# A two-layer graph attention kernel: the attention products ahead of the scores in each turn

## The chip, the cores and the metric

The kernel runs on one core of a Trainium2 chip. The metric is the device time of one execution in microseconds (us); the median of several runs is used. Every core has the same engines: TensorE (PE in the profile; its weight loads are listed as PEld), VectorE (DVE), ScalarE (ACT), GpSimd (POOL) and SyncE (SP), which issues all the transfers here. Each engine works through its own list of instructions in order, and semaphores tie the lists together.

## The reference

The input x holds 128 graphs of 128 nodes with 512 features, in fp32; adj is a Boolean adjacency matrix for each graph. Two layers follow one another, each with a residual and a layer norm:

```
x = layernorm(x + attention0(x, adj))                    # 4 heads of 64, q/k/v from x, output Wo and bias
x = layernorm(x + attention1(layernorm'(x), adj | eye))  # 8 heads of 64, pre-norm with gamma, beta
```

In both, attention is softmax(mask(q k^T / 8)) v for each head, and then the output projection. Masked positions get a very negative value.

## The kernel before

**Work and turns.** The graphs are taken in 64 groups of two (`G = 2`). The groups pass through a software pipeline: `step(s)` is one turn, and holds work of five groups at once. In turn s, layer 0 makes q, k and v for group s (`product_0`), masks and softmaxes the scores of group s-1 ("part 0"), multiplies the probabilities of group s-2 with its values and makes its output projection (`out_product(0, s-2, ...)`); layer 1 makes q and k for s-2 (`qk`) and v for s-3 (`v`), softmaxes the scores of s-3 ("part 1" and "part 2", one for each of its two graphs), and makes the attention product and the output projection of group s-4 (`out_product(1, s-4, ...)`). The full set of this work stands in the turns s = 4 to 63; `opening`, two `closing` turns and `last` surround them.

**The order is written by hand.** The kernel is in manual-schedule mode: each engine executes its instructions in the order in which the calls stand in `step`. So the place of a call in `step` decides what an engine does next, and what stands behind an instruction that waits.

**Products.** All large projections use a scheme of seven products in place of eight (numbered 1 to 7 in `product`, `product_0` and `out_product`). Sums of input halves are made on GpSimd (`halves_sums`, L285). Several products accumulate in the same bank one after another, and after each one the partial sum is read by another engine. The table that says where each number goes:

```
INTO = {1: ("a", True), 2: ("c", True), 6: ("a", False), 5: ("f", True), 7: ("a", False),
        4: ("a", False), 3: ("f", False)}
```

Products 1, 6, 7 and 4 share one bank, 5 and 3 share another, 2 has one of its own. In `product_0` (matmuls at L378), products 1, 6 and 5 are copied away by ScalarE (L387), product 4 by ScalarE too (L389), and 2, 7 and 3 are added by VectorE (L392). In `out_product` (matmuls at L416) every product is added into the residual row r by VectorE (L420), and the next product of that bank must wait for this read. The `qk` and `v` products (L322) are handled by `taken` (ScalarE L348 and L350, VectorE L353).

**Banks.** PSUM, where TensorE writes, has eight banks here: four in a rotating pool (`mm_tile`, tag "mm"), and four with fixed tags: "a", "f", "a0" and "f0". `product_0` uses a0 and f0; `qk` and `v` use a and f; `out_product` uses a and f in layer 0, a0 and f0 in layer 1. Before the change, part 1 of the scores is written to a0 and f0, and the attention products of parts 0 and 1 to a and f.

**Softmax.** `scores` makes the score matmuls of all three parts (L449, L455; 64 active rows of the array). `masked` copies them to tiles that hold the mask's value (VectorE, L483), `maxima` takes the maxima of the rows (VectorE, L489), `exps` the exponentials with their sums (ScalarE, L498, four heads to a call for one half), `normalised` the reciprocals (VectorE, L506) and the scaling (GpSimd, L507). `blocks` and `probs_arrive` transpose the probabilities through VectorE (L522) and a trip to memory and back (L197, L203). `attend` multiplies them with the values (L568; 64 active columns) and copies the product to the tile aT (ScalarE, L571 and L573).

**Norms.** `stats` collects mean and variance on VectorE (L600, L601), `roots` computes the scale and the shift on GpSimd (L608 to L623), and appends the norm itself (ScalarE, L634) to a list; `flush()` in `step` emits what is on the list. `turn` transposes the normed rows for layer 1, again through VectorE (L212) and memory; the fetched tile is finished by ScalarE (L251). For layer 0 the same is done with the input, finished in `in_order` (ScalarE, L239).

Of the kernel before, what the change touches and what calls it, by code (L numbers as in the profile page):

```python
# [10 lines left out]
F32 = mybir.dt.float32  # L11
# [6 lines left out]
P = 128  # L18
# [9 lines left out]
def kernel(ctx: ExitStack, tc: tile.TileContext, x, adj, wq, wk, wv, wo, bo,  # L28
# [16 lines left out]
    ps_st = ctx.enter_context(tc.tile_pool(name="ps_st", bufs=1, space=PSUM))  # L45
# [4 lines left out]
    def mm_tile(name):  # L50
        return ps_mm.tile([P, 512], F32, tag="mm", name=name)
# [4 lines left out]
    def flush(what=later):  # L56
        while what:
            what.pop(0)()
# [16 lines left out]
    def load(g):  # L75
        if g >= NG:
            return
        R[g] = six.tile([P, G, E], F32, tag="r", name=f"r_{g}")
        M[g] = six.tile([P, G, N], U8, tag="m", name=f"m_{g}")
        nc.sync.dma_start(R[g], x[g * G:(g + 1) * G].rearrange("b n e -> n b e"))  # L80
        nc.sync.dma_start(M[g], adj[g * G:(g + 1) * G].rearrange("b i j -> i b j"))
# [191 lines left out]
    def sums(l, g):  # L273
        if not 0 <= g < NG:
            return
        xs = XS[l, g] = one.tile([P, 4, KH, N], F32, tag=f"xs{l}", name=f"xs{l}_{g}")
        halves_sums(xs, XT[l, g].rearrange("p (h c) (b n) -> p b h c n", h=2, b=2))

    def halves_sums(xs, a):
        s1, s2, s3, s4 = (xs[:, i] for i in range(4))  # L280
        for o, a0, a1, op in ((s1, a[:, 1, 0], a[:, 1, 1], ALU.add),
                              (s2, s1, a[:, 0, 0], ALU.subtract),
                              (s4, a[:, 0, 1], s2, ALU.subtract),
                              (s3, a[:, 0, 0], a[:, 1, 0], ALU.subtract)):
            nc.gpsimd.tensor_tensor(o, a0, a1, op=op)  # L285
# [142 lines left out]
    def group_of(s, part):  # L428
        g = s - (3 if part else 1)
        return g if 0 <= g < NG else None  # L430

    def scores(s):

        made = {}
        for part in PARTS:
            g = group_of(s, part)
            if g is None:
                continue
            if part == 1:
                ps = [ps_st.tile([P, 512], F32, tag=t, name=f"sc{part}_{g}_{t}") for t in ("a0", "f0")]  # L440
            else:
                ps = [mm_tile(f"sc{part}_{g}_{i}") for i in range(2)]
            ps = [x.rearrange("p (k n) -> p k n", n=N) for x in ps]
            if part == 0:
                for b in range(G):
                    for h in range(HEADS[0]):
                        r = slice((h % 2) * D, (h % 2 + 1) * D)
                        q_, k_ = (QKV[g][r, b, h // 2, i, :] for i in range(2))
                        nc.tensor.matmul(ps[h % 2][:, b * K0 + h // 2, :], q_, k_, start=True, stop=True)  # L449
            else:  # L450
                t = slice((part - 1) * N, part * N)
                for h in range(HEADS[1]):
                    r = slice((h % 2) * D, (h % 2 + 1) * D)
                    q_, k_ = (QK[1, g][r, i * K1 + h // 2, t] for i in range(2))
                    nc.tensor.matmul(ps[h % 2][:, h // 2, :], q_, k_, start=True, stop=True)  # L455
            made[part] = ps
        return made
# [13 lines left out]
    def masked(made, s, *parts):  # L471
        for part in parts:
            g = group_of(s, part)
            if g is None:
                continue
            for i in range(2):
                if part == 0:
                    mask = M[g][:, :, None, :].to_broadcast([P, G, K0, N])
                    o, sc = (x.rearrange("p (b k) n -> p b k n", b=G) for x in (SM[0][:, i], made[0][i]))
                else:  # L480
                    mask = M[g][:, part - 1, None, :].to_broadcast([P, K1, N])
                    o, sc = SM[part][:, i], made[part][i]
                nc.vector.copy_predicated(o, mask, sc)  # L483
# [8 lines left out]
    def exps(s, part, *halves):  # L492
        if group_of(s, part) is None:
            return
        sm, nmax, total = SM[part], NMAX[part], TOTAL[part]
        for i in halves:
            for k in range(K1):
                nc.scalar.activation(sm[:, i, k, :], sm[:, i, k, :], AF.Exp, bias=nmax[:, i, k:k + 1],  # L498
                                     accum_out=total[:, i, k:k + 1])
# [45 lines left out]
    def attend(s, *parts):  # L545

        for part in parts or PARTS:
            l = min(part, 1)
            g = s - (2, 4)[l]
            if not 0 <= g < NG:  # L550
                continue
            K = (K0, K1)[l]
            if part != 2:
                AT[l, g] = one.tile([P, G, K, N], F32, tag=f"aT{l}", name=f"aT{l}_{g}")
            pT = PT.pop((g, part))
            if part == 2:
                pm = mm_tile(f"av{part}_{g}")
            else:
                pm = ps_st.tile([P, 512], F32, tag="af"[part], name=f"av{part}_{g}")
            pm = pm.rearrange("p (k n) -> p k n", n=N)  # L560

            for b in range(G) if l == 0 else (part - 1,):
                for h in range(HEADS[l]):
                    i, kk = h % 2, h // 2
                    at = b * K0 + kk if l == 0 else kk
                    v = (QKV[g][:, b, kk, 2, i * D:(i + 1) * D] if l == 0
                         else V[1, g][:, b, h * D:(h + 1) * D])
                    nc.tensor.matmul(pm[i * D:(i + 1) * D, at, :].rearrange("p (a r) -> p a r", r=32), v,  # L568
                                     pT[:, :, i * K1 + at, :], start=True, stop=True)
            if l == 0:  # L570
                nc.scalar.copy(AT[l, g].rearrange("p b k n -> p (b k) n"), pm)  # L571
            else:
                nc.scalar.copy(AT[l, g][:, part - 1], pm)  # L573
# [155 lines left out]
    def step(s):  # L729

        direct = s in (2, 3)
        made = scores(s)
        load(s + 1)
        if s > 2:
            in_order(s)
            sums(0, s)
        masked(made, s, 0, 1, 2)
        attend(s)
        maxima(s, 0)
        if s > 3:  # L740
            maxima(s, 1)
        out_sums(0, s - 2)
        exps(s, 0, 0)
        product_0(s, 1)
        exps(s, 0, 1)
        out_product(0, s - 2, 1, 2, 5)
        if s == 3:
            maxima(s, 1)
        maxima(s, 2)
        product_0(s, 2)  # L750
        normalised(s, 0)
        out_product(0, s - 2, 6, 3)
        exps(s, 1, 0)
        stats(0, s - 2, 0)
        product_0(s, 6)
        exps(s, 1, 1)
        out_product(0, s - 2, 7)
        product_0(s, 5)
        out_product(0, s - 2, 4)
        stats(0, s - 2, 1)  # L760
        exps(s, 2, 0)
        product_0(s, 7)
        exps(s, 2, 1)
        normalised(s, 1)
        product_0(s, 3)
        blocks(s, 0)
        flush()
        product_0(s, 4)
        if direct:
            prepare(len(setup))  # L770
        else:
            turn(1, s - 2)
        out_sums(1, s - 4)
        v(s - 3, 1, 2)
        out_product(1, s - 4, 1)
        if not direct:
            arrive(1, s - 2)
        blocks(s, 1)
        probs_arrive(s, 0)
        v(s - 3, 6, 5)  # L780
        out_product(1, s - 4, 2)
        normalised(s, 2)
        v(s - 3, 7, 3)
        turn(0, s + 1)
        v(s - 3, 4)
        flush(latest)
        cleared(s + 1, 0, 1)
        if direct:
            finish_direct(s - 2)
        else:  # L790
            finish(s - 2, 0)
        if s == 2:
            weight_sums(w1qk, wsqk, 1)
        out_product(1, s - 4, 6, 5)
        if not direct:
            finish(s - 2, 1)
        out_product(1, s - 4, 7, 3, 4)
        blocks(s, 2)
        probs_arrive(s, 1)
        stats(1, s - 4, 0)  # L800
        stats(1, s - 4, 1)
        arrive(0, s + 1)
        probs_arrive(s, 2)
        cleared(s + 1, 2)
        addend(0, s - 1)
        with_self(s - 2)
        qk(s - 2, 1, 2, 6)
        flush()
        qk(s - 2, 5)
        addend(1, s - 3)  # L810
        qk(s - 2, 7, 3, 4)
        if s == 2:
            weight_sums(w1v, wsv, 0, 1)
        if s == 3:
            weight_sums_out(1)
# [130 lines left out]
```

## Time and profile before

| | before |
|---|---|
| time, median of 3 runs | 2787.71 us (2786.65 to 2788.02) |
| span of the profiled execution | 2784.5 us |
| TensorE matmuls, busy | 2768.7 us (99%) |
| TensorE weight loads, busy | 2609.6 us (94%) |
| VectorE, busy | 1795.3 us (64%) |
| GpSimd, busy | 1747.4 us (63%) |
| ScalarE, busy | 1502.0 us (54%) |
| transfers | 405.24 MB, mean 146 GB/s |
| granted TensorE clock | 1.000 |

How to read it: a busy share is the time in which an engine executed something, over the span. Matmuls overlap one another, so their busy time says that TensorE had work, not that it was at its peak. The timeline lists an engine's instructions by start time, merged where equal ones follow one another; "x16" counts hardware records, of which each fp32 matmul here has two. A bracket at the end of a row gives the idle time ahead of it and whose work ended it. The list of waits sums such idle times by pairs.

### The profile page before, as it was taken

The page shows a single profiled execution, that of the slowest core. Times are in us where ns is not written, and L with a number is a line of the kernel's source. Part 1 is how long each engine was busy: PE and PEld are TensorE (multiplying, and loading weights), DVE is VectorE, ACT ScalarE, POOL GpSimd, SP SyncE. Part 2 cuts the span into 40 slices and gives each one's busy share as a digit, 9 for nine tenths or more (in the row PEclk, how much of TensorE's full clock was granted, in tenths as well). Part 3 has the DMA queues.
Part 4 walks back from the last instruction along what each step waited for, and adds up shares of the span by engine and source line. Part 5 has one row for each costly group of instructions (what it writes and reads, how often), then busy time and mean ns, then how long its engine had stood idle before and what let it go on. Part 6 is the DMA issues. An engine that isn't in the chain of part 4 may idle for free.

```text
span 2784.5 us, 63222 instructions
## 1 busy us (share of the span) xinstructions
PE 2768.7 (99%) x23317; PEld 2609.6 (94%) x23317; DVE 1795.3 (64%) x3307; ACT 1502.0 (54%) x4811; POOL 1747.4 (63%) x2307
## 2 busy tenths in 40 slices
PE   8999999999999999999999999999999999999998
PEld 8999999999999999999999999999999999999997
DVE  5766666666666666666666666666666666666665
ACT  3555555645555556455555564555555645555554
POOL 4566566666665666666656666666566666666664
PEclk9999999999999999999999999999999999999999
DMA  5355454464454544645545445455454464554532
GB/s 169 109 144 165 129 165 148 127 176 140 143 165 128 166 148 127 179 137 143 164 127 168 147 129 175 139 145 165 127 167 146 129 177 135 147 163 128 160 107 69
DMA packets 281796, 405.24 MB, mean 146 GB/s; under 512 B 44680, under 2 KB 206480, under 8 KB 281488
## 3 DMA queue, kind: packets, MB, share of 16 engines
q1 hardware_dynamic: 281488, 401.20, 49.2%
q8 instruction: 185, 3.03, 0.5%
q14 instruction: 123, 1.01, 0.1%
HBM read 205.00 MB, written 196.08 MB: 144 GB/s over the span
## 4 chain that ended last, share of the span: by engine, by line
PE 96%; DVE 1%; issue 0%; POOL 0%; DMA 0%; ACT 0%; SPq 0%; POOLq 0%; ACTq 0%; DVEq 0%
PE qka L322 16%; PE a L378 12%; PE oa L416 12%; PE qkf L322 8%; PE va L322 8%; PE av L568 6%; PE f L378 6%; PE of L416 6%; PE qkc L322 4%; PE vf L322 4%; PE c L378 3%; PE oc L416 3%; PE sc L449 2%; PE sc L455 2%; PE vc L322 2%; PE sc_a L455 2%
## 5 line engine op out<-in xcount | busy, mean ns | idle before, releaser
L507 POOL TENSOR_TENSOR sm<-sm,rec 128x1024 f32<-128x1024 f32 x192 | 364.1, 1896 | 383.1 <-DVE rec L506 382.7
L498 ACT ACTIVATE sm<-sm,nmax 128x128 f32<-128x128 f32 x1536 | 595.4, 394 | 4.6 <-DVE nmax L489 3.7
L589 POOL TENSOR_TENSOR r<-r,bias 128x1024 f32<-128x1024 f32 x128 | 302.2, 2361 | 63.5 <-ACT r L588 63.5
L420 DVE TENSOR_TENSOR r<-oa,r 128x256 f32<-128x256 f32 x508 | 212.1, 418 | 200.3 <-PE oa L416 192.7
L285 POOL TENSOR_TENSOR xs<-xT 128x256 f32<-128x256 f32 x256 | 188.7, 737 | 218.3 <-ACT xT L239 165.1
L498 ACT ACTIVATION_READ_ACCUMULATOR sm<-sm,nmax 128x1 f32 x1536 | 295.9, 193 | 0.0
L348 ACT COPY eqk<-qka 128x512 f32<-128x512 f32 x128 | 74.9, 585 | 349.2 <-PE qka L322 349.2
L483 DVE COPY_PREDICATED sm<-m,sc 128x512 f32<-128x512 uint8 x256 | 172.8, 728 | 135.4 <-PE sc L449 134.9
L322 PE MATMUL qka<-xs,wsqk 128*128 128x128 f32 x2048 | 249.7, 275 | 0.1
L322 PE MATMUL qkf<-xs,w 128*128 128x128 f32 x2048 | 249.8, 275 | 0.0
L522 DVE STREAM_TRANSPOSE turnedp<-sm 128x1024 f32<-128x1024 f32 x189 | 233.9, 1238 | 15.2 <-DMA scrp<-turnedp 10.9
L322 PEld LDWEIGHTS qka<-xs,wsqk 128*128 128x128 f32 x2048 | 239.0, 192 | 0.3 <-POOL xs L285 0.3
L322 PEld LDWEIGHTS qkf<-xs,w 128*128 128x128 f32 x2048 | 239.0, 192 | 0.0
L353 DVE TENSOR_TENSOR qk<-qka,eqk 128x512 f32<-128x512 f32 x64 | 44.3, 691 | 290.4 <-PE qka L322 290.4
L489 DVE TENSOR_REDUCE nmax<-sm 128x8 f32<-128x1024 f32 x192 | 226.2, 1205 | 0.1
L416 PE MATMUL oa<-wso,so 128*128 128x256 f32 x760 | 206.0, 380 | 0.7 <-DVE r L420 0.7
L416 PE MATMUL of<-wo,so 128*128 128x256 f32 x760 | 205.5, 379 | 0.0
L608 POOL TENSOR_SCALAR ve<-mv 128x2 f32<-128x2 f32 x191 | 41.0, 214 | 261.5 <-DVE mv L601 255.4
L634 ACT ACTIVATE r<-r,shift,root 128x512 f32<-128x512 f32 x254 | 192.4, 807 | 8.7 <-POOL shift L623 4.7
L469 POOL MEMSET sm<- 128x1024 f32 x192 | 178.8, 951 | 0.0
L600 DVE BATCH_NORM_STATS2 st<-r 128x6 f32<-128x512 f32 x254 | 171.6, 676 | 4.4
L416 PEld LDWEIGHTS of<-wo,so 128*128 128x128 f32 x760 | 144.2, 190 | 19.9
(155 smaller groups left out, 6801.4 us busy)
## 6 DMA issues: line engine op xcount, KB each, us to landing
scrp<-turnedp SPq DMA_DIRECT2D x189, 512.0 KB, 3.2
pT<-scrp SPq DMA_DIRECT2D x756, 128.0 KB, 4.0
scr<-turned SPq DMA_DIRECT2D x121, 512.0 KB, 4.4
raw<-scr SPq DMA_DIRECT2D x484, 128.0 KB, 3.6
r<-in_x_dram SPq DMA_DIRECT2D x64, 512.0 KB, 3.9
out_dram<-r SPq DMA_DIRECT2D x63, 512.0 KB, 4.9
m<-in_adj_dram SPq DMA_DIRECT2D x64, 32.0 KB, 3.6
raw_r<-in_L_gnn_w_qkv_dram SPq DMA_DIRECT2D x8, 256.0 KB, 4.1
```

What stands on the lines that cost most here:

```text
L285: nc.gpsimd.tensor_tensor(o, a0, a1, op=op)
L322: nc.tensor.matmul(o, lhsT, rhs, start=first and n == 0, stop=n == len(todo) - 1, skip_group_check=True)
L378: nc.tensor.matmul(acc[:, t * P:(t + 1) * P], lhsT, rhs, start=first and n == 0, stop=n == len(todo) - 1, skip_group_check=True)
L416: nc.tensor.matmul(acc, left[:, c], right[:, c], start=first and c == 0, stop=c == hk - 1, skip_group_check=True)
L420: nc.vector.tensor_add(part, acc, part)
L469: nc.gpsimd.memset(sm, NEG1 if part else NEG0)
L489: nc.vector.tensor_reduce(NMAX[part], SM[part], AX.X, ALU.max, negate=True)
L498: nc.scalar.activation(sm[:, i, k, :], sm[:, i, k, :], AF.Exp, bias=nmax[:, i, k:k + 1], accum_out=total[:, i, k:k + 1])
L507: nc.gpsimd.tensor_tensor(SM[part], SM[part], rec[:, :, :, None].to_broadcast([P, 2, K1, N]), op=ALU.mult)
L522: nc.vector.transpose(t.rearrange("p q (h r) -> p q h r", r=32), SM.pop(part).rearrange("p i k (q r) -> p q (i k) r", r=32))
L589: nc.gpsimd.tensor_tensor(R[g], R[g], (bias0, bias1)[l][:, None, :].to_broadcast([P, G, E]), op=ALU.add)
L634: nc.scalar.activation(R[g][:, b], R[g][:, b], AF.Identity, bias=shift[:, b:b + 1], scale=root[:, b:b + 1])
```

## The change

Three edits:

1. In `step`, `attend(s)` is moved ahead of `scores(s)`. On TensorE the attention products of a turn then come first, and the scores after them. `load`, `in_order` and `sums` move ahead of both; `masked` stays behind `scores`. `opening`, `closing` and `last` keep their order.
2. The fixed banks are exchanged to go with it: part 1 of the scores goes to a and f, the attention products of parts 0 and 1 go to a0 and f0. That applies to all turns.
3. The last four exponentials of part 2, `exps(s, 2, 1)`, move from ahead of `normalised(s, 1)` to behind `flush()`. On ScalarE the norm of layer 0's rows (L634) then stands ahead of these four exponentials, and the copy of `product_0`'s fourth product (L389) still stands behind both.

The aim of the first two is to have the attention products, and with them the copies to aT and the sums made of those, early in the turn; the aim of the third is to have the norm's rows early for the transposition that follows.

```diff
@@ scores @@
             if part == 1:
-                ps = [ps_st.tile([P, 512], F32, tag=t, name=f"sc{part}_{g}_{t}") for t in ("a0", "f0")]
+                ps = [ps_st.tile([P, 512], F32, tag=t, name=f"sc{part}_{g}_{t}") for t in "af"]
@@ attend @@
-                pm = ps_st.tile([P, 512], F32, tag="af"[part], name=f"av{part}_{g}")
+                pm = ps_st.tile([P, 512], F32, tag=("a0", "f0")[part], name=f"av{part}_{g}")
@@ step @@
         direct = s in (2, 3)
-        made = scores(s)
         load(s + 1)
         if s > 2:
             in_order(s)
             sums(0, s)
+        attend(s)
+        made = scores(s)
         masked(made, s, 0, 1, 2)
-        attend(s)
         maxima(s, 0)
...
         exps(s, 2, 0)
         product_0(s, 7)
-        exps(s, 2, 1)
         normalised(s, 1)
         product_0(s, 3)
         blocks(s, 0)
         flush()
+        exps(s, 2, 1)
         product_0(s, 4)
```

## The prediction

> **What bounds the kernel now.** I read the page first, then the list of who waited for whom on TensorE, then the timeline of one turn in the steady middle (turn s starts at 1437.20 us, the next at 1480.04: a period of 42.84 us), engine by engine. Columns of the timeline: start, duration, engine, line, operation, count, and in brackets the idle time before it with its releaser.
>
> ```profile
> PE 2768.7 (99%) x23317; PEld 2609.6 (94%) x23317; DVE 1795.3 (64%) x3307; ACT 1502.0 (54%) x4811; POOL 1747.4 (63%) x2307
> PEld a L378 <- ACT aT L573: 10.3, 60, 0.2
> ```
>
> The second line is the longest of the waits: 10.3 us in all, 60 times, 0.2 us at most. TensorE is never short of work: nothing it waits for in the middle of the run exceeds 0.2 us, so the time is that of its instruction list. The change adds and removes no work there. It can gain only what TensorE idles, and it can lose wherever it makes TensorE wait. The slack of the other engines therefore decides.
>
> ```profile
> 1437.20 1.16 PE L449 MATMUL sc<-qkv 64*128 64x128 f32 x16
> 1440.08 1.09 PE L568 MATMUL av<-pT,qkv 128*64 128x128 f32 x16
> 1442.85 1.16 PE L378 MATMUL a<-xT,w 128*128 128x128 f32 x8
> 1446.92 0.60 PE L416 MATMUL oa<-wso,so 128*128 128x256 f32 x2
> 1447.36 0.59 PE L416 MATMUL of<-wo,so 128*128 128x256 f32 x2
> 1449.13 0.60 PE L416 MATMUL oa<-wso,so 128*128 128x256 f32 x2
> 1450.90 0.60 PE L416 MATMUL oa<-wso,aT 128*128 128x256 f32 x2
> 1457.08 1.03 PE L416 MATMUL oa<-wo,aT 128*128 128x256 f32 x4
> ```
>
> The turn opens with scores (2.88 us to 1440.08), then the attention products (2.77 us to 1442.85), then layer 0's products in fixed order. Products 6, 3, 7 and 4 of the layer-0 output (starts 1446.92, 1447.36, 1449.13, 1450.90) reuse two banks, so each needs VectorE to have read the former partial sum. The last row is layer 1's first output product, which needs bank a0.
>
> ```profile
> 1438.45 1.36 DVE L483 COPY_PREDICATED sm<-m,sc 128x512 f32<-128x512 uint8 x2 [2.23 <-PE sc L449]
> 1442.15 2.34 DVE L489 TENSOR_REDUCE nmax<-sm 128x8 f32<-128x1024 f32 x2
> 1444.99 0.42 DVE L420 TENSOR_TENSOR r<-oa,r 128x256 f32<-128x256 f32 x1 [0.50 <-PE oa L416]
> 1446.19 1.21 DVE L489 TENSOR_REDUCE nmax<-sm 128x8 f32<-128x1024 f32 x1
> 1447.89 0.37 DVE L420 TENSOR_TENSOR r<-oa,r 128x256 f32<-128x256 f32 x1
> 1449.76 0.42 DVE L420 TENSOR_TENSOR r<-oa,r 128x256 f32<-128x256 f32 x1
> 1451.53 0.42 DVE L420 TENSOR_TENSOR r<-oa,r 128x256 f32<-128x256 f32 x1 [1.35 <-PE oa L416]
> ```
>
> This is what the page's 64% hides. From the first scores (1438.45) to 1450.18 VectorE works without a pause but for 0.50 us: six masked copies, two maxima, then reads of the output banks. Its share is low over the turn, but here it is a queue with little to spare.
>
> ```profile
> 1452.99 0.19 POOL L608 TENSOR_SCALAR ve<-mv 128x2 f32<-128x2 f32 x1 [3.04 <-DVE mv L601]
> 1454.33 0.22 POOL L623 TENSOR_SCALAR shift<-shift 128x2 f32<-128x2 f32 x1
> 1454.75 1.51 ACT L634 ACTIVATE r<-r,shift,root 128x512 f32<-128x512 f32 x2
> 1456.16 0.46 ACT L389 COPY qkv<-a 128x384 f32<-128x384 f32 x1
> ```
>
> ScalarE reaches the norms (L634) at the moment when the shift that they need is there (1454.55), because eight exponentials filled the time until then. L389, which frees bank a0, follows them.
>
> **What the Trainium skill says.** "PSUM — Partial Sum Buffer", section "Engine vs sequencer instructions", says "ScalarE/VectorE/GpSimdE queues are strict FIFO" and that matmuls start in program order. The trace agrees: each engine's rows stand in the order of the code. So an operation that waits holds back everything behind it. "TensorEngine Tiling (Array Packing)", section "Key Properties", says "Mode switching requires drain". The trace agrees: starts lie 0.112 us apart within full-array matmuls, but 0.205 us apart across the step to the half-row scores.
>
> **The change part by part.**
>
> *Order on TensorE.* Scores and attention products swap places. The work is the same, and there are three mode switches a turn before and after. Extra time over the steady spacing, from the starts of the first instructions after each: full to rows 0.19 us, rows to columns 0.13, columns to full 0.19, sum 0.51. After: full to columns 0.14 (seen in the last turn), rows to full 0.19 (seen once in the opening), columns to rows unseen. I bound that by 0.1 and 0.3 and take 0.19, as for the other switch into rows: sum 0.52. I count it as nothing (at the ends, -0.1 to +0.1 us a turn).
>
> *Banks.* Part 1's scores move from a0/f0 to a/f, the attention products the other way. Banks a and f are free by 1437.9, when ScalarE's copy L350 has read a, and a0/f0 since layer 1's last output read. New waits: oa (1444.29) for the masked copy of part 1, and a0's next product for ScalarE's aT copy. With all of VectorE's masks shifted as below, bank a is read by 1443.2, in time, and the aT copy ends near 1439.5. The last scores share a buffer with the last attention product; its copy ends near 1440.8, before they start. The attention products also need the probabilities 2.88 us sooner: the last fetch is issued by 1475.68 and lands 4.0 us later (median), 1479.7, against 1481.9. All hidden.
>
> *Masks behind the attention products.* The first scores now come 2.77 us later, so VectorE starts at 1441.22 instead of 1438.45, and idles until then. All its following work stays in the same order: masks 3.70 us to 1444.92, two maxima 2.34 to about 1447.18 (an overlap of 0.08 off). Then three reads, no longer waiting for TensorE: starts 1447.18, 1447.66, 1448.00, and the third maximum at 1448.33, 2.14 later than before. The reads behind it keep their distances to that maximum (1.70 us and 3.57 us): product 6's at 1450.03, product 7's at 1451.90. A TensorE wait released by VectorE ends about 0.06 us after the read (from the closing turns, where 2736.46 released 2736.52). So:
> - product 6: 1447.60 + 0.06 = 1447.66, 0.74 late;
> - product 3: 1448.42 + 0.06, 1.12 late;
> - product 7: 1450.40 + 0.06, 1.33 late;
> - product 4: 1452.32 + 0.06 = 1452.38, 1.48 late.
>
> These are totals, not to be added. A first matmul after a wait has no weights loaded ahead; the closing turns show 1.13 instead of 1.03 us for such four, so 0.10 more: 1.58 us a turn. From product 4's read on VectorE waits for TensorE again and the delay stops growing. Exponentials also start 2.77 later, but bank a0 is read by e1 at about 1448.2, before product 6 of the projections (1449.0), so that is hidden.
>
> *Last four exponentials behind the norm.* ScalarE finishes the first four of part 2 at about 1455.06. The norms now stand next and wait for the shift. Product 4 to norm start took 1454.75 - 1450.90 = 3.85 us, set by the sum, statistics and GpSimd's chain, and those stay. Then norms 1.41, four exponentials 1.54, L389 0.46: L389 ends 7.26 us after product 4's start. TensorE reaches layer 1's first output product 1457.08 - 1450.90 = 6.18 after it. Its wait is 7.26 + 0.06 - 6.18 = 1.14, plus 0.10 for the restart: 1.24 us. Behind L389 stand the copies of the values' projections, but these are needed only 0.86 us later. An earlier norm would serve the transposition of layer 1's input; that is not on TensorE's path, as its xT copies end before their products.
>
> *Sum.* 1.58 + 1.24 = 2.82 us a turn. Both waits need turns with all three parts and layer-1 outputs, s = 4 to 63: 60 turns, 169 us. The rest of the turn is led by TensorE and only shifts. 2787.7 + 169 = 2957 us.
>
> **The rivals.**
> - *Only one of the two.* For: the norms could be ready sooner than I think. Against: their chain is measured, from product 4 on. The masks alone: 60 x 1.58 = 95, 2883 us; the norms alone: 74, 2862 us. Chance 0.09.
> - *A further wait joins.* For: e5's copy frees f0 at 1453.7 against a need of 1454.3, slack 0.6, and the worst probability landing is 5.6 us, slack 0.6 too. Another 0.8 us a turn gives 3005 us. Chance 0.08.
> - *All hidden.* For: VectorE 64%, ScalarE 54% busy. Against: 2.77 us of shift meets 0.50 + 1.1 us of slack at product 6. 2788 us. Chance 0.03.
> - *Faster.* The switches get cheaper, or the earlier aT copies end small waits: at most 0.17 us x 60 = 10, 2777 us. Against: that 0.17 is the switch itself, as 1442.85 is long after all its data. Chance 0.02.
>
> **How the numbers follow.** The main case keeps 0.78. Without restart costs and with switches 0.1 cheaper it is 2.82 - 0.30 = 2.52 a turn, 2939; with 0.1 dearer switches and half the further wait, 3.3, 2986. Rounded outward to take a little of both neighbours: 2925 to 2990. Faster 0.02, same 0.03, slower 0.95.
>
> **What would show it.** Right: a period near 45.7 us; TensorE near 94% busy; in its waits, output products released by VectorE's read L420 (some 85 us in all) and by ScalarE's L389 (some 70); VectorE idle about 5.0 us before the first mask; ScalarE idle about 1.2 us before L634, released by GpSimd. Wrong: a period of 43, or waits on DMA or on the scores' banks. If L389 doesn't appear, the second part fails; if L420 doesn't, the first.

## The result, and the profile after

| | before | after |
|---|---|---|
| time, median | 2787.44 us | 2944.62 us |
| period of a turn in the middle | 42.84 us | 45.45 us |
| TensorE matmuls, busy | 2768.7 us | 2826.4 us |

The ratio of the times is 1.0565 (95% interval 1.0552 to 1.0578): the change costs 157 us. The forecast was 2957 us. The period is the distance between the first matmuls of successive turns, the median over the run; 60 turns times 2.61 us make 156 of the 157 us.

The list of waits on TensorE in the kernel after (total, times, longest) names two releasers that held TensorE in no full turn before:

```profile
PE oa L416 <- ACT qkv L389: 49.6, 60, 0.8
PE oa L416 <- DVE r L420: 38.8, 61, 1.0
PE of L416 <- DVE r L420: 11.5, 60, 0.2
```

Both appear in 60 turns, as they must if only the full turns pay. Their sum, 99.9 us, is less than what was lost, and TensorE's busy time rose although its matmuls are the same 23317. "Perfetto Trace Analysis", section "Tensor Engine Instruction (MATMUL, LD_WEIGHTS)", says that a matmul's end is an estimate; here the modelled end of the matmul ahead of a gap reaches 0.16 us into the gap, which is booked as work (0.379 us of duration against 0.217 us between starts, in the 256-column products). So I measure by starts. TensorE's timeline of one turn after, from 1428.15 us; the rows that answer to those shown of before:

```profile
1428.15 1.09 PE L568 MATMUL av<-pT,qkv 128*64 128x128 f32 x16
1430.92 1.16 PE L449 MATMUL sc<-qkv 64*128 64x128 f32 x16
1433.80 1.16 PE L378 MATMUL a<-xT,w 128*128 128x128 f32 x8
1438.66 0.67 PE L416 MATMUL oa<-wso,so 128*128 128x256 f32 x2 [0.63 <-DVE r L420]
1439.52 0.67 PE L416 MATMUL of<-wo,so 128*128 128x256 f32 x2 [0.19 <-DVE r L420]
1441.51 0.67 PE L416 MATMUL oa<-wso,so 128*128 128x256 f32 x2
1443.36 0.60 PE L416 MATMUL oa<-wso,aT 128*128 128x256 f32 x2
1450.52 1.13 PE L416 MATMUL oa<-wo,aT 128*128 128x256 f32 x4 [0.82 <-ACT qkv L389]
```

Up to 1433.80 nothing is lost: 5.65 us, as before (1437.20 to 1442.85). By product 4 (1443.36) the turn is 1.51 us late, by layer 1's first output product (1450.52) 2.50, and with that product's restart 2.61 (medians over the middle of the run). The rest of the turn only shifts. Product 7 (1441.51) carries no bracket although it starts 0.22 us later than product 3 led to: 0.07 us of this is product 3's restart, and the modelled end hides a wait as short as the other 0.15. The queue that holds the first three, VectorE's timeline in the same turn:

```profile
1432.16 1.35 DVE L483 COPY_PREDICATED sm<-m,sc 128x512 f32<-128x512 uint8 x2 [5.01 <-PE sc L449]
1435.87 2.31 DVE L489 TENSOR_REDUCE nmax<-sm 128x8 f32<-128x1024 f32 x2
1438.11 0.41 DVE L420 TENSOR_TENSOR r<-oa,r 128x256 f32<-128x256 f32 x1
1439.29 1.21 DVE L489 TENSOR_REDUCE nmax<-sm 128x8 f32<-128x1024 f32 x1
1440.99 0.37 DVE L420 TENSOR_TENSOR r<-oa,r 128x256 f32<-128x256 f32 x1
1442.76 0.39 DVE L420 TENSOR_TENSOR r<-oa,r 128x256 f32<-128x256 f32 x1
1443.99 0.42 DVE L420 TENSOR_TENSOR r<-oa,r 128x256 f32<-128x256 f32 x1 [0.84 <-PE oa L416]
```

The idle time ahead of the first mask grew from 2.23 to 5.01 us. From there to 1443.15 it works without a pause; the 0.50 us of slack ahead of the first read is gone. And ScalarE and GpSimd, around the norms of the same turn:

```profile
1446.79 0.22 POOL L623 TENSOR_SCALAR shift<-shift 128x2 f32<-128x2 f32 x1
```

```profile
1447.05 1.52 ACT L634 ACTIVATE r<-r,shift,root 128x512 f32<-128x512 f32 x2 [1.03 <-POOL shift L623]
1450.02 0.46 ACT L389 COPY qkv<-a 128x384 f32<-128x384 f32 x1
```

ScalarE now idles until the shift is there, and between the norms and L389 stand four exponentials (1448.48 to 1450.02). L389 ends at 1450.48 and releases TensorE at 1450.52.

The weight loads of the same turn show how the two kinds of wait end, at product 6 and at layer 1's first output product:

```profile
1438.63 0.30 PEld L416 LDWEIGHTS oa<-wso,so 128*128 128x128 f32 x2 [0.79 <-issue]
1450.52 0.73 PEld L416 LDWEIGHTS oa<-wo,aT 128*128 128x128 f32 x4 [1.23 <-ACT qkv L389]
```

Neither has its weights loaded ahead. Ahead of product 6's load the list has a semaphore instruction of its own (PEldq in the view of line L416, from 1438.3 to 1438.8 us):

```profile
L416 PEldq EVENT_SEMAPHORE  x1: 51/51/51, 1438.6 to 1438.6; - x1
```

VectorE's read ends at 1438.52, the load starts at 1438.63, and the matmul at 1438.66. At the other product the load itself waits for L389, and load and matmul start together at 1450.52.

### The profile page after: what moved, and what is told of

The parts are those of the page before. It is cut to its first block, busy times and chain, and to the rows that moved or that the text cites. A ratio compares the mean times of both kernels' runs of the same rounds, so it can differ in the third digit from the quotient of the medians.

```text
span 2942.7 us, 63165 instructions
## 1 busy us (share of the span) xinstructions
PE 2826.4 (96%) x23317; PEld 2608.7 (89%) x23317; DVE 1774.2 (60%) x3307; ACT 1491.9 (51%) x4811; POOL 1743.0 (59%) x2307
## 5 line engine op out<-in xcount | busy, mean ns | idle before, releaser
L420 DVE TENSOR_TENSOR r<-oa,r 128x256 f32<-128x256 f32 x508 | 209.7, 413 | 146.6 <-PE oa L416 140.6
L416 PE MATMUL oa<-wso,so 128*128 128x256 f32 x760 | 214.7, 391 | 38.8 <-DVE r L420 38.8
L634 ACT ACTIVATE r<-r,shift,root 128x512 f32<-128x512 f32 x254 | 193.0, 808 | 71.5 <-POOL shift L623 67.5
L416 PE MATMUL of<-wo,so 128*128 128x256 f32 x760 | 210.2, 385 | 12.0 <-DVE r L420 11.5
L416 PEld LDWEIGHTS oa<-wso,so 128*128 128x128 f32 x760 | 129.9, 189 | 74.5 <-issue 49.0
L416 PEld LDWEIGHTS of<-wo,so 128*128 128x128 f32 x760 | 139.1, 189 | 51.7 <-issue 34.1
```

Source lines behind the costliest of these rows:

```text
L416: nc.tensor.matmul(acc, left[:, c], right[:, c], start=first and c == 0, stop=c == hk - 1, skip_group_check=True)
L420: nc.vector.tensor_add(part, acc, part)
L634: nc.scalar.activation(R[g][:, b], R[g][:, b], AF.Identity, bias=shift[:, b:b + 1], scale=root[:, b:b + 1])
```

## The experiments

Three explanations stood against each other. The *queue theory*: two separate delays, one in VectorE's queue and one in ScalarE's, each reaching TensorE by a wait of its own. The *common cause*: one delay, of VectorE, that drags the norm along, so that the place of the exponentials matters little. The *TensorE theory*: the new order or the new banks cost time on TensorE itself. "Turn" is the period less 42.84 us. Each ratio is to executions of the kernel before in the same series (median 2786.70 us for the first four rows, 2787.01 for the others).

| experiment | time, us | ratio to before (95% interval) | turn, us | expected by the queue theory, us |
|---|---|---|---|---|
| order and banks | 2878.73 | 1.033 (1.0316 to 1.0344) | +1.51 | 2878 |
| exponentials only | 2853.05 | 1.0239 (1.0225 to 1.0253) | +1.10 | 2853 |
| banks only | 2787.77 | 1.0005 (0.9996 to 1.0013) | 0.00 | 2787 to 2790 |
| order, old banks | 2923.3 | one run | +2.25 | 2923 |
| exponentials behind the copy | 2816.43 | 1.0106 (1.0092 to 1.0119) | +0.49 | 2817 |
| part 0 first | 2796.11 | 1.0033 (1.002 to 1.0046) | +0.15 | 2795 |
| parts 0 and 1 first | 2827.57 | 1.0146 (1.0131 to 1.0162) | +0.65 | 2822 |
| maxima moved | 2821.18 | 1.0121 (1.0108 to 1.0135) | +0.54 | 2804 |

**Order and banks.** The changed kernel with the last exponentials in their old place:

```diff
         product_0(s, 7)
+        exps(s, 2, 1)
         normalised(s, 1)
...
         flush()
-        exps(s, 2, 1)
         product_0(s, 4)
```

> The attention products first and the banks exchanged, the last exponentials left in their old place. Queue theory (VectorE's masks start 2.77 us late and the reads behind them hold TensorE; the exponentials ahead of the copy L389 are a second, separate wait): the changed kernel's turn is 1.51 us longer by product 4, and that alone stays: 60 x 1.51 = 91, about 2878 us; no wait for L389. Rival (one common cause: whatever delays VectorE delays the norm too, and the place of the exponentials matters little): about 2930 to 2945 us. Rival (TensorE itself: dearer switches of the array's mode or of banks): TensorE's waits stay small and the loss stands in the starts around the scores.

Measured: 2878.73 us, and the wait for L389 is gone from the list. VectorE's part alone is worth 91 us.

**Exponentials only.** The kernel before with edit 3 alone:

```diff
         product_0(s, 7)
-        exps(s, 2, 1)
         normalised(s, 1)
...
         flush()
+        exps(s, 2, 1)
         product_0(s, 4)
```

> The kernel before with only the last four exponentials moved behind the norm. Queue theory: the copy L389 ends 7.12 us after product 4's start (norm 3.70 after it, 1.43 + 1.54 + 0.46 for norms, exponentials and copy), TensorE is there after 6.18 us, with 0.05 for the signal and 0.10 for the restart 1.09 us a turn: 60 x 1.09 = 65, about 2853 us, all of it as waits for L389. Rival (common cause): without VectorE's delay the norm is early enough and the time stays at 2788 us.

Measured: 2853.05 us. ScalarE's timeline of one turn:

```profile
1445.76 1.52 ACT L634 ACTIVATE r<-r,shift,root 128x512 f32<-128x512 f32 x2 [1.28 <-POOL shift L623]
1448.72 0.46 ACT L389 COPY qkv<-a 128x384 f32<-128x384 f32 x1
```

and TensorE's:

```profile
1442.06 0.60 PE L416 MATMUL oa<-wso,aT 128*128 128x256 f32 x2
1449.23 1.13 PE L416 MATMUL oa<-wo,aT 128*128 128x256 f32 x4 [0.83 <-ACT qkv L389]
```

The same 3.70 us from product 4 to the norm as in the kernel after, without any delay on VectorE. The two parts add up, 91 + 66 = 157 us, which is the whole change; a common cause would have made one of them nearly nothing. (Both are taken from 2787.44 us, as the 157 are.)

**Banks only.** Order and exponentials as before, edit 2 alone:

```diff
-                ps = [ps_st.tile([P, 512], F32, tag=t, name=f"sc{part}_{g}_{t}") for t in ("a0", "f0")]
+                ps = [ps_st.tile([P, 512], F32, tag=t, name=f"sc{part}_{g}_{t}") for t in "af"]
...
-                pm = ps_st.tile([P, 512], F32, tag="af"[part], name=f"av{part}_{g}")
+                pm = ps_st.tile([P, 512], F32, tag=("a0", "f0")[part], name=f"av{part}_{g}")
```

> Only the four fixed banks exchanged, the order of before. Queue theory: bank a is read by ScalarE 0.7 us into the turn and part 1's scores come at 1.0 us, so nothing waits: 2787 to 2790 us. Rival (TensorE and banks): the new holders of a and f collide with the layer-0 output products, at least 0.5 us a turn: 2818 us or more.

Measured: 2787.77 us; the interval holds 1. The exchange costs nothing by itself.

**Order, old banks.** Edit 1 alone: order and banks with the two bank lines as before.

```diff
-                ps = [ps_st.tile([P, 512], F32, tag=t, name=f"sc{part}_{g}_{t}") for t in "af"]
+                ps = [ps_st.tile([P, 512], F32, tag=t, name=f"sc{part}_{g}_{t}") for t in ("a0", "f0")]
...
-                pm = ps_st.tile([P, 512], F32, tag=("a0", "f0")[part], name=f"av{part}_{g}")
+                pm = ps_st.tile([P, 512], F32, tag="af"[part], name=f"av{part}_{g}")
```

> The attention products first, but in their old banks a and f, exponentials in their old place. Queue theory: the first attention product must wait until ScalarE's L350 has read the last layer-1 query/key product out of bank a, 0.75 us into the turn, and that wait comes on top of the 1.51 us: 2.26 x 60 = 136, about 2923 us. Rival (the exchange is not needed): 2878 us, as with the exchanged banks.

Measured: 2923.3 us in one run. Its waits on TensorE:

```profile
PE av L568 <- ACT qk L350: 41.2, 61, 0.7
PE a L378 <- DVE sm L483: 19.6, 61, 0.7
PE oa L416 <- DVE r L420: 14.8, 61, 0.7
PE of L416 <- DVE r L420: 11.4, 60, 0.2
```

The time was as expected, and the first wait too. The second was not in my expectation: product 1 of the projections must wait until bank a0's scores are masked. It adds nothing, because TensorE then has less to wait for at L420 (14.8 for 38.4 us): VectorE's queue sets the end of the chain wherever TensorE meets it first.

**Exponentials behind the copy.** The kernel before with the four exponentials behind L389:

```diff
         product_0(s, 7)
-        exps(s, 2, 1)
         normalised(s, 1)
...
         flush()
         product_0(s, 4)
+        exps(s, 2, 1)
```

> The kernel before with the last four exponentials one place further back still: behind the copy L389. Queue theory: L389 now ends 19.3 us into the turn, in time for 19.9, but the next copy of a value product (L348) stands behind the exponentials and ends at 21.1, against 20.75: 0.40 us of wait and 0.10 for the restart, 60 x 0.50 = 30, about 2817 us; no wait for L389, all of it for L348. Rival (the exponentials cost time wherever they stand behind the norm): about 2853 us as in the run with the exponentials alone. Rival (only L389 matters): 2787 us.

Measured: 2816.43 us. TensorE's waits:

```profile
PE va L322 <- ACT ev L348: 15.0, 62, 1.1
```

The wait moved from L389 to the next copy in the queue, and shrank by what lies between the two. What costs is the copy behind the exponentials, whichever it is.

**Part 0 first, and parts 0 and 1 first.** How much of the shift is free? Order and banks, with the attention products divided:

```diff
-        attend(s)
+        attend(s, 0)
         made = scores(s)
         masked(made, s, 0, 1, 2)
+        attend(s, 1, 2)
```

> Only part 0's attention product ahead of the scores, parts 1 and 2 behind; banks exchanged, exponentials in their old place. VectorE's masks start 1.0 us late instead of 2.77. Queue theory: the slack takes it: product 4's needed read ends at 13.3 us against 13.8, no wait for L420; there is one more switch of the array's mode, 0.13 us a turn, 62 turns: about 2795 us. Rival (loss in proportion to the shift): 1.0 / 2.77 x 91 = 33 and the switch, about 2829 us.

```diff
-        attend(s)
+        attend(s, 0, 1)
         made = scores(s)
         masked(made, s, 0, 1, 2)
+        attend(s, 2)
```

> Parts 0 and 1 of the attention product ahead of the scores, part 2 behind. The masks start 1.9 us late. Queue theory: product 3 waits 0.14 us and product 7 0.11, each with a restart of 0.10: 0.45 us a turn, and the switch 0.13: 27 + 8 = 35, about 2822 us. Rival (in proportion): 62 + 8 = 70, about 2857 us.

Measured: 2796.11 and 2827.57 us. In the first, no wait for L420 beyond those of the closing turns: 1.0 us of shift goes into the slack, and the 0.15 us a turn is the additional switch of the array's mode: the scores and attention products take 5.80 us for 5.65. In the second, one turn on TensorE:

```profile
1425.01 0.60 PE L416 MATMUL oa<-wso,so 128*128 128x256 f32 x2
1425.65 0.67 PE L416 MATMUL of<-wo,so 128*128 128x256 f32 x2
1427.64 0.67 PE L416 MATMUL oa<-wso,so 128*128 128x256 f32 x2
1429.48 0.60 PE L416 MATMUL oa<-wso,aT 128*128 128x256 f32 x2
```

Product 3 (1425.65) starts 0.21 us later than product 6 (1425.01) led to, product 7 0.14 later than product 3 and its restart of 0.07 led to; product 6 itself doesn't wait. That they wait and product 6 doesn't is as expected, the time is 5 us over: each wait ends 0.15 us after the read, where I had put 0.06. Shifts of 1.0, 1.9 and 2.77 us cost 0.00, 0.50 and 1.51 us of waits a turn: a threshold, not a proportion.

**Maxima moved.** The same order on TensorE as in order and banks, but VectorE's queue rearranged:

```diff
-        masked(made, s, 0, 1, 2)
+        masked(made, s, 0)
         maxima(s, 0)
-        if s > 3:
-            maxima(s, 1)
+        masked(made, s, 1, 2)
...
         out_product(0, s - 2, 1, 2, 5)
-        if s == 3:
-            maxima(s, 1)
-        maxima(s, 2)
+        maxima(s, 1)
...
         out_product(0, s - 2, 7)
+        maxima(s, 2)
         product_0(s, 5)
```

> The attention products all first and the banks exchanged, exponentials in their old place, and VectorE's queue rearranged: part 0's maxima right behind its own masks, part 1's behind the first three output reads, part 2's behind product 7's read. The work is the same. Queue theory: the output reads come about 1.1 us earlier; only product 7 still waits, 0.17 us and 0.10 for the restart: 60 x 0.27 = 16, about 2804 us. Rival (the loss belongs to the new order on TensorE, not to VectorE's queue): 2878 us, as with order and banks alone.

Measured: 2821.18 us. VectorE's queue, not the order on TensorE, makes the loss: with the same list of matmuls 58 of the 91 us are gone. It missed the expected 2804. The wait that I missed stands in the list of the weight loads; in that of the matmuls the modelled ends hide all but one of its times:

```profile
PEld oa L416 <- DVE sm L483: 15.9, 61, 0.6
```

Part 0's maxima, now ahead of part 1's masks, hold back the mask that frees bank a, and layer 0's first output product waits for it: 0.23 us longer than before, and 0.10 for the restart. I had looked at the reads and not at this bank. Product 7 waits 0.13 us and 0.07. Together 0.53 of the 0.54 us a turn.

The changed kernel does get what the three edits were meant to bring, but nothing on TensorE was waiting for it. ScalarE starts the first copy to aT 1.63 us into the turn in place of 4.02. The norms start 18.91 us into the turn, against 19.31 with order and banks alone; edit 3 alone brings 17.40 for 17.56. For these 0.40 and 0.16 us the copy L389 ends 1.15 and 1.40 us later.

No experiment beats the kernel before. Its TensorE waits for nothing longer than 0.2 us in the middle, so a new order with the same switches of the array's mode has next to nothing to gain there; what is left is the 0.51 us a turn at the three mode switches, and I tried nothing against it.

## Why the prediction was right

- *TensorE is the bound and can only lose*: right. The switches cost the same in both orders: the block of scores and attention products takes 5.65 us either way, so the unseen switch from columns to rows costs what I took for it.
- *Banks hidden*: right, by the run with the banks alone. The probabilities, needed 2.88 us sooner, are in time: no wait on a transfer in the full turns.
- *Masks behind the attention products, 1.58 us*: the mechanism right, 1.51 measured, by balancing errors. The release after a read takes 0.15 us, not 0.06, at products 6, 3 and 7: a semaphore instruction stands ahead of their weight loads, and the closing turn's wait that gave the 0.06 has none. So the totals at products 6, 3 and 7 are 0.80, 1.22 and 1.44 us in place of 0.74, 1.12 and 1.33. The restart costs 0.07, not 0.10. And product 4 doesn't wait at all: product 7's read stood 0.10 us closer behind the statistics (0.02 us of pause before, an overlap of 0.08 after), ended at 15.01 us into the turn, and product 7's own wait and restart had already delayed product 4 to 15.21. That the sum came within 0.07 us is in part luck.
- *Exponentials behind the norm, 1.24 us*: 1.09 measured. The mis-sized term is the 3.85 us from product 4 to the norms, which I took as set by the sum, the statistics and GpSimd. Before, the norms started at 1454.75 and the shift had been there since 1454.55: ScalarE, still busy with exponentials, held them for about 0.16 of the 3.85 us. Freed of four of them it starts after 3.70 us.
- *Sum, 2.82 us a turn*: 2.61. The two errors of 0.07 and 0.15 make, unrounded, 0.21 x 60 = 13 us, the distance of 2957 from 2944.6.
- *The rivals*: "only one of the two" falls, as each part alone costs its share and they add up; "a further wait" didn't appear; "all hidden" and "faster" fall with the times. The 1.1 us that I set against "all hidden" at product 6 is the slack of product 3; product 6 had 1.5 us between the read's end (1445.41) and its start (1446.92), and 0.50 + 1.5 us is still less than 2.77.
- *What would show it*: period, VectorE's 5.01 us and ScalarE's 1.03 us of idleness came as said. The sums of the waits (50 and 50 us for 85 and 70) and TensorE's share (96% for 94%) did not, because part of each gap, and the longer restart, is booked as busy. I should have named the starts as the test.

## What to carry to other kernels

Here one engine was at its limit, and a new order of its own work gained nothing by itself. In such a case, look at what the order does to the queues of the others, and how much pause each has between the point that is delayed and the point where the full engine needs it back. A low busy share over the whole turn says nothing of this: VectorE was at 64% and had 0.5 us to spare just there. And in a queue that runs strictly in order, an operation that must wait belongs behind the work that fills its waiting time, and short copies that free banks belong ahead of long work.

## What the runs showed of the hardware

- A TensorE wait for a VectorE read ended 0.15 us after the read where a semaphore instruction stood ahead of the weight load (medians over the middle of the kernel after: 0.04 us to that instruction, 0.08 to the load, 0.03 to the matmul), and the restart then cost 0.07 us. It ended 0.04 to 0.06 us after the releasing operation where the weight load itself waited, for ScalarE (L389 ended 1450.48, matmul 1450.52) or for VectorE (maxima moved: mask ended 1418.52, matmul 1418.58), and the restart cost 0.10 us. That the semaphore instruction makes the difference is read from the traces; no run took it away.
- One more switch between the array's column and row modes in a turn costs 0.15 us (part 0 first: period 42.99 against 42.84 us). The three switches of a turn cost the same whether rows or columns come first (5.65 us for the block in both). The traces show the longer spacing of the starts at a switch, not what causes it.
